# Graph network on one Trainium2 core: the convolution weights' transform with five channels per row block, a separate tile for its difference, and a later fetch of the gates' weights

## The chip, the cores and the metric

The kernel runs on one core of one Trainium2 chip. The metric is the device time of one execution in microseconds (us). TensorE (PE in the profile) multiplies, VectorE (DVE), ScalarE (ACT) and GpSimd (POOL) do the elementwise work, SyncE (SP) issues most loads. Each engine runs its own queue strictly in order; engines meet at semaphores.

## What is computed

The input is 64 graphs of 256 nodes with 256 features each, and a 256x256 adjacency matrix per graph. Layer 0 is a normalised graph convolution with a residual and a layer norm. Layer 1 is, for each graph:

```python
h      = relu(bn1(conv1d(x, conv1_w)))            # one tap
h      = bn2(conv1d(h, conv2_w, pad=8))           # 17 taps, 256 -> 256 channels
x_conv = relu(h + x)
A      = exp(-dist(x @ w_se.T)) * adj
x_nmp  = A @ relu(x @ w_msg.T + b_msg)
x_out  = GRU(input=[x_conv, x_nmp], state=x)      # w_ih, w_hh: the gates
x      = layernorm(x + x_out)
```

Everything is float32. The 17-tap convolution along the nodes is done in frequency space: blocks of 32 nodes, transforms of length 48, one 256x256 matrix of weights per frequency. Only the transform of those weights is touched by the change, apart from the place of one fetch.

## The kernel before, in words

The graphs are taken in four sets of 16 (`Q = 16`, `NQ = 4`). For each set the function `graphs` runs layer 0 and the first part of layer 1 for one graph after another; then `products` multiplies the spectra of all 16 graphs with the weights of each frequency, an inverse transform follows, and `gates` runs the GRU.

The first set has an extra load: while its 16 graphs run, `weights` transforms the 17 taps of `conv2_w` into 24 real frequency rows (`NU = 24`). The taps are put on the partitions: `GC = 4` groups of 64 input channels (`GW = 64`), 17 taps each, so 68 rows (`KT`). A matrix `dft_w` of 68 x 96 columns (24 frequencies x 4 groups), once for the cosine half and once for the sine half, multiplies them. One call of `weights` treats four channels of each group (1024 columns); 16 calls, one per graph, cover all 64. In each call:

- `load_taps` (line 248) fetches the next part into one of two `taps` buffers, with five transfers on SP's queue (lines 257, 258);
- DVE multiplies the taps by the batch-norm scale (line 265);
- PE makes `p_u`, four products of 256 columns for each half (line 272), and ACT copies them into `u_set` (line 275);
- POOL forms the sum of the two halves (line 277) in a third tile, DVE writes the difference over the second tile (line 278), and so has to wait until POOL has read it;
- POOL issues three stores to `ud` in HBM (line 280), 384, 368 and 384 KB.

The generator `weights` yields twice, and `graphs` runs its first half after the transposes of the graph (`p_x1T`, line 387) and its second half after `p_dist` (line 455), by the table `PLACES`. The order of source lines is not the last word: the framework schedules the recorded instructions onto the queues, with priorities and its own idea of when each is ready, and may move an instruction ahead where its inputs permit. Then the order on each engine is fixed.

Other lines that the steps below touch: `layernorm` (lines 290 to 304: DVE statistics, a `pow` on POOL at 293, DVE at 301, ACT at 303), `layer0` (POOL `pow` for the degrees at 329, POOL bias add at 351, DVE at 372), `layer1` (ACT relu of `h` at 400, PE `p_dft` at 431, DVE `dist_r` at 448, PE `p_dist` at 455, DVE `aT` at 457, PE `p_nmp` at 462), `load_u` (line 478, six buffers of 256 KB), `input_sums` (POOL, lines 737 to 740) and `gate_weights` (lines 887, 889, 894). The pools `ustream` and `gate` are opened after the pool `setup` is closed and take over its memory, so their first loads wait for the last users of the setup tiles, among them the `bih` and `bhh` tiles, which reuse the `taps` buffers.

Of the kernel before, what the change touches and what calls it, by code (L numbers as in the profile page):

```python
# [9 lines left out]
F32 = mybir.dt.float32  # L10
AF = mybir.ActivationFunctionType
ALU = mybir.AluOpType
AX = mybir.AxisListType

P = 128
# [11 lines left out]
def kernel(  # L27
# [27 lines left out]
    nc = tc.nc  # L55
    B, N, D = x.shape
    TAPS = conv2T.shape[1]
# [8 lines left out]
    Q = P // GT  # L66
# [3 lines left out]
    const = ctx.enter_context(tc.tile_pool(name="const", bufs=1))  # L70
# [45 lines left out]
    ident = const.tile([P, P], F32)  # L116
# [60 lines left out]
    NF = len(FREQ)  # L177
# [1 line left out]
    RE = (1, 4, 6, 8, 9, 10, 11) + tuple(range(16, 32))  # L179
    IM = (3, 5, 7, 12, 13, 14, 15) + tuple(range(32, 48))  # L180
    NU = NF + 1
    GC = 4
    GW = D // GC
    KT = GC * TAPS
    TR = 16

# [3 lines left out]

    ud = [dram.tile([NU * GC, GW, D], F32, name=f"ud{i}") for i in range(3)]
    fwd = const.tile([P, GT // 2 + 2, FL], F32)
    dft_w = const.tile([KT, 2, NU, GC], F32)

    def tables(pool):
        period = pool.tile([1, 25 * FL], F32, name="period")
        for k in range(FL):
            nc.vector.memset(period[:, k::FL], math.cos(2 * math.pi * k / FL))

        def wave(f, sine, n):  # L200

            first = 0 if not sine else (3 * FL // 4 if f > 0 else FL // 4)
            return period[:, first : first + abs(f) * (n - 1) + 1 : abs(f)]

        fwd_row = pool.tile([1, FL, FL], F32, name="fwd_row")
        w_row = pool.tile([1, TAPS, 2, NU], F32, name="w_row")
        zeros = pool.tile([NT, FL * fm_rows // NT], F32, name="zeros")
        nc.gpsimd.memset(zeros, 0.0)
        nc.gpsimd.dma_start(fm.rearrange("(p r) f -> p (r f)", p=NT), zeros)

        for r in range(2):
            nc.vector.memset(w_row[:, :, r, NF], 0.5)
        nc.vector.memset(w_row[:, 1::2, 1, NF], -0.5)
        for n, f in enumerate(FREQ):
            nc.vector.tensor_copy(w_row[:, :, 0, n], wave(f, False, TAPS))
            nc.vector.tensor_copy(w_row[:, :, 1, n], wave(f, True, TAPS))

        wd = dram.tile([TAPS, 2 * NU], F32, name="wd")
        nc.sync.dma_start(wd.unsqueeze(0), w_row.rearrange("p t h n -> p t (h n)"))
        wt = pool.tile([KT, 2 * NU], F32, name="wt")  # L220
        for c in range(GC):
            nc.sync.dma_start(wt[c * TR : (c + 1) * TR], wd[:TR])
        nc.sync.dma_start(wt[GC * TR :], bcast_rows(wd[TR], 2 * NU, GC))
        mask = pool.tile([KT, GC], F32, name="mask")
        nc.vector.tensor_reduce(
            mask[: GC * TR], ident[: GC * TR, : GC * TR].rearrange("p (c t) -> p c t", c=GC), AX.X, ALU.add
        )
        nc.vector.tensor_copy(mask[GC * TR :], ident[GC * TR : KT, GC * TR : KT])
        nc.vector.tensor_mul(
            dft_w.rearrange("p h n c -> p (h n) c"), wt.unsqueeze(2).to_broadcast([KT, 2 * NU, GC]),  # L230
            mask.unsqueeze(1).to_broadcast([KT, 2 * NU, GC]),
        )

        for r in range(2):
            nc.vector.memset(fwd_row[:, :, 2 * r], 1.0)
        nc.vector.memset(fwd_row[:, 1::2, 2], -1.0)
        for n, f in enumerate(FREQ):
            nc.vector.tensor_copy(fwd_row[:, :, RE[n]], wave(f, False, FL))
            nc.vector.tensor_copy(fwd_row[:, :, IM[n]], wave(-f, True, FL))
        nc.sync.dma_start(fm[fm0 : fm0 + FL].unsqueeze(0), fwd_row)  # L240
        for j in range(GT // 2 + 2):

            first = fm0 + PAD - NT * (j - 1)
            nc.sync.dma_start(fwd[:, j, :], fm[first : first + P])

    TAPS_OF = {}

    def load_taps(pool, n, parts):

        if n == parts:  # L250
            return
        ng = GW // parts
        tp = TAPS_OF[n] = pool.tile([KT, ng, D], F32, name="taps", bufs=2)

        taps = conv2T.rearrange("(c g) t o -> c t g o", c=GC)[:, :, n * ng : (n + 1) * ng]
        for c in range(GC):
            nc.sync.dma_start(tp[c * TR : (c + 1) * TR], taps[c, :TR])
        nc.sync.dma_start(tp[GC * TR :], taps[:, TR])

    def weights(pool, n, parts, scale):  # L260

        ng = GW // parts
        load_taps(pool, n + 1, parts)
        tp = TAPS_OF.pop(n)
        nc.vector.tensor_mul(tp, tp, scale[:KT].unsqueeze(1).to_broadcast([KT, ng, D]))
        m, mf = NU * GC, NF * GC
        us = [pool.tile([m, ng, D], F32, name=f"u_set{i}", bufs=2) for i in range(3)]
        for i in range(2):
            for j in range(0, ng, 2):
                p = accbank("p_u").rearrange("p (g o) -> p g o", g=2)  # L270
                for h in range(2):
                    nc.tensor.matmul(
                        p[:m, h], dft_w[:, i].rearrange("p n c -> p (n c)"), tp[:, j + h], start=True, stop=True
                    )
                nc.scalar.copy(us[i][:, j : j + 2], p[:m])
            if i == 1:
                nc.gpsimd.tensor_tensor(us[2][:mf], us[0][:mf], us[1][:mf], op=ALU.add)
                nc.vector.tensor_sub(us[1][:mf], us[1][:mf], us[0][:mf])
                for d, u, rows in zip(ud, us, (m, m, mf)):
                    nc.gpsimd.dma_start(d[:rows, n * ng : (n + 1) * ng], u[:rows])  # L280
            yield

    def layernorm(y, engine, eps=LN_EPS):
# [192 lines left out]
    def load_u(n, i):  # L476
        u = ustream.tile([P, DCH, D], F32, name="u")
        nc.sync.dma_start(
            u, ud[i][n * GC : (n + 1) * GC].rearrange("c g o -> (c g) o").rearrange("(k p) o -> p k o", p=P)
        )  # L480
        return u

# [385 lines left out]
    with tc.tile_pool(name="setup", bufs=1) as setup:  # L868
        norms = batch_norms(setup)
        next(norms)  # L870
        load_taps(setup, 0, Q)
        nc.sync.dma_start(bmsg_t, bcast_rows(b_msg, D))
        nc.sync.dma_start(bc1[:, D:], bcast_rows(b_se, NSE))
        run(merge(layer0(0), layer0(1)))
        scale2 = next(norms)
        tables(setup)
        load(2)

        def gate_weights():
            for b, half_inputs, cols in ((B11, 0, 0), (T1, 0, 1), (B21, 1, 0), (B22, 1, 1)):  # L880
                at = slice(cols * D, (cols + 1) * D)
                if half_inputs == 0:
                    parts = ((slice(0, DCH), w_hhT), (slice(DCH, HALF), w_ihT[D : D + P]))
# [12 lines left out]

        others = [weights(setup, i, Q, scale2) for i in range(Q)]
        more_weights = gate_weights()
        for i in range(4, 7):
            others[i] = chain(others[i], take(more_weights, 1))  # L900
        run(graphs(0, range(Q), V, others))
        bih_t = setup.tile([P, 3 * D], F32, name="bih", tag="taps", bufs=2)
        nc.sync.dma_start(bih_t, bcast_rows(b_ih, 3 * D))
        bhh_t = setup.tile([P, 3 * D], F32, name="bhh", tag="taps", bufs=2)
        nc.sync.dma_start(bhh_t, bcast_rows(b_hh, 3 * D))
        brz = brz_t.rearrange("p i d -> p (i d)")
        nc.vector.tensor_add(brz, bih_t[:, : 2 * D], bhh_t[:, : 2 * D])
# [127 lines left out]
```

## Time and profile before

| what | value |
|---|---|
| time, median of 3 | 2213.34 us (2213.03 to 2220.08) |
| profiled span | 2214.4 us, granted PE clock 0.986 |
| PE busy | 2077.4 us, 94% of the span |
| DVE / ACT / POOL busy | 71% / 38% / 30% |
| first set of graphs, from first `p_x1T` to `p_x1T` of graph 16 | 36.27 to 345.91 us |
| PE matmul records of `p_u` | 256, of 9853 in all |

Each fp32 matmul of the source stands as two records in the trace, so the 128 products of `p_u` are 256 records. A line of the timeline gives start and duration in us, engine, source line, the operation with its tiles, and in brackets how long the engine sat idle before it and what ended the wait. The sixteen starts of `p_x1T` are used below as the marks that part one graph from the next.

### The profile page before, as it was taken

Reading aid. Unit: us, or ns where it says so; the run is one execution under the profiler, and the core shown is the slowest. Engines: PE = TensorE matmul, PEld = TensorE weight load, DVE = VectorE, ACT = ScalarE, POOL = GpSimd, SP = SyncE. Lnnn points to the kernel's source line nnn. Section 1 sums busy time; section 2 is a strip of 40 time slices with the busy share of each in tenths; the row PEclk is TensorE's granted clock in tenths of the full one; section 3 lists DMA queues with packets and bytes.
Section 4 is the critical chain, followed back from the end, with each engine's and each line's share of the span. In section 5 each row is a group of like instructions: output and inputs, shape, how many; then the busy total and the mean of one; then the engine's idle time right before and its main releaser. Section 6 shows DMA issues by size and latency. Waiting matters only on the chain.

```text
span 2214.4 us, 29080 instructions
## 1 busy us (share of the span) xinstructions
PE 2077.4 (94%) x9853; PEld 1753.5 (79%) x9853; DVE 1564.9 (71%) x3749; ACT 835.9 (38%) x1850; POOL 670.2 (30%) x653
## 2 busy tenths in 40 slices
PE   5999989969999998999999998899999999889998
PEld 4777767848888886788888887688888887678887
DVE  6655448794657899855556989955555879987666
ACT  3555533435441122446543122445554112222222
POOL 2333331113231233322322233321331123344442
PEclk9999999989999999999999999999999999999999
DMA  3655467544337644424334754433323754444342
GB/s 108 193 166 169 150 193 258 170 134 115 118 92 214 200 138 116 132 86 124 105 106 148 214 160 125 143 96 105 119 87 113 216 171 114 115 120 113 102 110 57
DMA packets 251424, 305.20 MB, mean 138 GB/s; under 512 B 18602, under 2 KB 230074, under 8 KB 251275
## 3 DMA queue, kind: packets, MB, share of 16 engines
q1 hardware_dynamic: 183180, 199.85, 29.2%
q10 hardware_dynamic: 45280, 68.04, 8.7%
q0 software_dynamic: 22816, 35.45, 8.1%
q8 instruction: 78, 1.28, 0.2%
q14 instruction: 70, 0.57, 0.1%
HBM read 200.71 MB, written 102.57 MB: 137 GB/s over the span
## 4 chain that ended last, share of the span: by engine, by line
PE 50%; DVE 13%; issue 6%; POOL 5%; ACT 4%; DMA 0%; ACTq 0%; POOLq 0%; SPq 0%; DVEq 0%
PE p_rz L756 18%; PE p_n L793 9%; PE p_k L486 8%; PE p_nmp L462 3%; PE p_out L368 2%; PE p_dft L431 2%; PE p_conv L396 2%; PE p_hT L358 2%; PE p_msg L417 1%; POOL sums L738 1%; POOL ln_rs L293 1%; PE p_dist L455 1%; POOL sums L740 1%; POOL sums L739 1%; DVE gn L798 1%
## 5 line engine op out<-in xcount | busy, mean ns | idle before, releaser
L756 PE MATMUL p_rz<-wrz,sums 128*128 128x256 f32 x1536 | 356.0, 383 | 19.5 <-DVE gn L798 9.8
L793 PE MATMUL p_n<-wn,inputs 128*128 128x256 f32 x1536 | 351.3, 381 | 16.3 <-DVE first L769 15.7
L756 PEld LDWEIGHTS p_rz<-wrz,sums 128*128 128x128 f32 x1536 | 288.6, 191 | 70.9 <-issue 15.8
L793 PEld LDWEIGHTS p_n<-wn,inputs 128*128 128x128 f32 x1536 | 285.7, 190 | 62.2 <-DVE first L769 18.9
L756 PE MATMUL p_rz<-wrz,inputs 128*128 128x256 f32 x1152 | 272.8, 380 | 2.1 <-ACT inputs L728 1.5
L293 POOL TENSOR_TENSOR ln_rs<-ln_rs,neg_half 128x2 f32<-128x2 f32 x129 | 100.4, 778 | 541.3 <-DVE ln_rs L292 455.7
L756 PEld LDWEIGHTS p_rz<-wrz,inputs 128*128 128x128 f32 x1152 | 216.8, 190 | 33.7 <-ACT inputs L728 3.6
L805 ACT ACTIVATE nn<-gn 128x256 f32<-128x256 f32 x128 | 53.2, 416 | 325.6 <-DVE gn L802 324.8
L486 PE MATMUL p_k<-u,VM 128*128 128x256 f32 x736 | 175.1, 380 | 0.8 <-DMA u<-ud 0.8
L329 POOL TENSOR_TENSOR dis<-deg,neg_half 128x2 f32<-128x2 f32 x64 | 49.9, 780 | 403.5 <-DVE deg L327 324.9
L303 ACT ACTIVATE x_g<-x_g,ln_mr,ln_rs 128x256 f32<-128x256 f32 x128 | 70.0, 593 | 256.1 <-DVE ln_mr L301 256.1
L486 PEld LDWEIGHTS p_k<-u,VM 128*128 128x128 f32 x736 | 138.3, 190 | 21.2 <-DMA u<-ud 2.2
L431 PE MATMUL p_dft<-fwd,h 128*128 128x240 f32 x512 | 118.2, 375 | 27.2 <-ACT h L400 27.2
L737 POOL TENSOR_TENSOR sums<-inputs 128x384 f32<-128x384 f32 x64 | 70.0, 1093 | 241.6 <-issue 172.0
L396 PE MATMUL p_conv<-wc,xn 128*128 128x259 f32 x512 | 128.1, 393 | 12.2 <-ACT xn L388 12.2
L358 PE MATMUL p_hT<-adjT,x 128*128 128x256 f32 x512 | 126.8, 392 | 10.0 <-DVE adjT L341 9.3
L431 PEld LDWEIGHTS p_dft<-fwd,h 128*128 128x128 f32 x512 | 95.9, 192 | 44.0 <-ACT h L400 36.4
L462 PE MATMUL p_nmp<-aT,msg 128*128 128x256 f32 x512 | 125.5, 389 | 5.0 <-DVE aT L457 5.0
L368 PE MATMUL p_out<-w,hT 128*128 128x256 f32 x512 | 124.4, 386 | 1.3 <-ACT hT L363 1.1
L396 PEld LDWEIGHTS p_conv<-wc,xn 128*128 128x128 f32 x512 | 98.0, 194 | 31.5 <-ACT xn L388 16.4
L351 POOL TENSOR_TENSOR x_t<-x_t,b_t 128x512 f32<-128x512 f32 x64 | 85.2, 1332 | 121.9 <-ACT x L350 93.2
L417 PE MATMUL p_msg<-wmsg,xn 128*128 128x256 f32 x512 | 122.0, 381 | 0.0
(153 smaller groups left out, 3880.0 us busy)
## 6 DMA issues: line engine op xcount, KB each, us to landing
u<-ud SPq DMA_DIRECT2D x284, 256.0 KB
xn_d<-xn ACTq DMA_DIRECT2D x64, 512.0 KB
inputs<-xn_d SPq DMA_DIRECT2D x64, 512.0 KB
adj_t<-in_adj_dram SPq DMA_DIRECT2D x64, 256.0 KB
x_t<-in_x_dram SPq DMA_DIRECT2D x64, 256.0 KB
x_d<-x ACTq DMA_DIRECT2D x64, 256.0 KB
x_g<-x_d SPq DMA_DIRECT2D x64, 256.0 KB
xc_d<-VM SPq DMA_DIRECT2D x64, 256.0 KB
```

The lines of the kernel that those rows point to most:

```text
L293: nc.gpsimd.tensor_tensor(rs[:, : len(chunks)], rs[:, : len(chunks)], neg_half[:, : len(chunks)], op=ALU.pow)
L303: nc.scalar.activation(y[:, c, :], y[:, c, :], AF.Identity, bias=mr[:, c : c + 1], scale=rs[:, c : c + 1])
L351: nc.gpsimd.tensor_tensor(x_t, x_t, b0_t.unsqueeze(1).to_broadcast([P, NCH, D]), op=ALU.add)
L358: nc.tensor.matmul(p[:, k, :], x1[:, mc, k * P : (k + 1) * P], adjT[:, mc, 1 - mc : 3 - mc, :].rearrange("p n q -> p (n q)"), start=mc == ...
L368: nc.tensor.matmul(p[:, c, :], hT[:, k, c * P : (c + 1) * P], w0[:, k, :], start=k == 0, stop=k == DCH - 1)
L396: nc.tensor.matmul(p, x1T[:, k, c * P : (c + 1) * P], wc1[:, k, :], start=k == 0, stop=k == DCH - 1)
L417: nc.tensor.matmul(p[:, c, :], x1T[:, k, c * P : (c + 1) * P], wmsg[:, k, :], start=k == 0, stop=k == DCH - 1)
L431: nc.tensor.matmul(p[:, t0 * FL : t1 * FL], h[:, c, k * P : (k + 1) * P], fwd[:, first : first + t1 - t0, :].rearrange("p t f -> p (t f)") ...
L462: nc.tensor.matmul(p[:, k, :], msg[:, mc, k * P : (k + 1) * P], aT[:, mc].rearrange("p n q -> p (n q)"), start=mc == 0, stop=mc == NCH - 1,)
L486: nc.tensor.matmul(p[:, j * D : (j + 1) * D], v[:, k, :], u[:, k, :], start=k == 0, stop=k == DCH - 1)
L756: nc.tensor.matmul(p[:, j * D : (j + 1) * D], a[:, k], wrz[:, b, k], start=k == 0, stop=k == HALF - 1)
L793: nc.tensor.matmul(p[:, o * D : (o + 1) * D], lhsT, w, start=j == 0, stop=j == len(part) - 1)
```

## The change

It puts five groups of 52 channels on the rows in place of four groups of 64 (85 rows in place of 68; 120 output rows in place of 96), so that 13 calls of `weights` suffice. The last group has only 48 channels left; its 13th part repeats channels that are not read back. The difference gets a tile of its own (`us[3]`), so DVE need not wait until POOL has read. All 120 rows of sum and difference are stored. To make the plain row (index `NF`) come out right from the difference, its coefficients become 0.5 and 1/0. `dft_w` moves from the constants into the setup pool. `load_taps` now issues seven transfers. The fetch and subtraction of the gates' weights, until now hung onto graphs 4 to 6, take the places 13 to 15, which have no part of `weights` left.

```diff
-    GC = 4
-    GW = D // GC
+    GC = 5
+    GW = 52
+    NPARTS = 13
...
-            nc.vector.memset(w_row[:, :, r, NF], 0.5)
-        nc.vector.memset(w_row[:, 1::2, 1, NF], -0.5)
+            nc.vector.memset(w_row[:, :, r, NF], (0.5, 1.0)[r])
+        nc.vector.memset(w_row[:, 1::2, 1, NF], 0.0)
...
-        ng = GW // parts
+        ng = GW // NPARTS
...
         for c in range(GC):
-            nc.sync.dma_start(tp[c * TR : (c + 1) * TR], taps[c, :TR])
-        nc.sync.dma_start(tp[GC * TR :], taps[:, TR])
+            nc.sync.dma_start(tp[c * TR : (c + 1) * TR], taps(c, 0, TR, 1))
+        nc.sync.dma_start(tp[GC * TR : KT - 1], taps(0, TR, GC - 1, GW * TAPS))
+        nc.sync.dma_start(tp[KT - 1 :], taps(GC - 1, TR, 1, 1))
...
-        us = [pool.tile([m, ng, D], F32, name=f"u_set{i}", bufs=2) for i in range(3)]
+        us = [pool.tile([m, ng, D], F32, name=f"u_set{i}", bufs=2) for i in range(4)]
...
-                nc.gpsimd.tensor_tensor(us[2][:mf], us[0][:mf], us[1][:mf], op=ALU.add)
-                nc.vector.tensor_sub(us[1][:mf], us[1][:mf], us[0][:mf])
-                for d, u, rows in zip(ud, us, (m, m, mf)):
-                    nc.gpsimd.dma_start(d[:rows, n * ng : (n + 1) * ng], u[:rows])
+                nc.vector.tensor_sub(us[3], us[1], us[0])
+                nc.gpsimd.tensor_tensor(us[2], us[0], us[1], op=ALU.add)
+                for d, u in zip(ud, (us[0], us[3], us[2])):
+                    nc.gpsimd.dma_start(d[:, n * ng : (n + 1) * ng], u)
...
-        others = [weights(setup, i, Q, scale2) for i in range(Q)]
         more_weights = gate_weights()
-        for i in range(4, 7):
-            others[i] = chain(others[i], take(more_weights, 1))
+        others = [weights(setup, i, scale2) for i in range(NPARTS)]
+        others += [take(more_weights, 1) for i in range(NPARTS, Q)]
```

More of the change, by code (lines that the diff above doesn't have):

```diff
@@ L192 @@
     fwd = const.tile([P, GT // 2 + 2, FL], F32)
-    dft_w = const.tile([KT, 2, NU, GC], F32)
+    DFT_W = {}
     def tables(pool):
@@ L224, in tables @@
         mask = pool.tile([KT, GC], F32, name="mask")
+        dft_w = DFT_W[0] = pool.tile([KT, 2, NU, GC], F32, name="dft_w")
         nc.vector.tensor_reduce(
-            mask[: GC * TR], ident[: GC * TR, : GC * TR].rearrange("p (c t) -> p c t", c=GC), AX.X, ALU.add
+            mask, ident[:KT, : GC * TR].rearrange("p (c t) -> p c t", c=GC), AX.X, ALU.add
         )
-        nc.vector.tensor_copy(mask[GC * TR :], ident[GC * TR : KT, GC * TR : KT])
+        nc.vector.tensor_add(mask, mask, ident[:KT, GC * TR : KT])
         nc.vector.tensor_mul(
@@ L246, with load_taps, taps, weights @@
     TAPS_OF = {}
-    def load_taps(pool, n, parts):
-        if n == parts:
+    def load_taps(pool, n):
+        if n == NPARTS:
             return
-        ng = GW // parts
+        ng = GW // NPARTS
         tp = TAPS_OF[n] = pool.tile([KT, ng, D], F32, name="taps", bufs=2)
-        taps = conv2T.rearrange("(c g) t o -> c t g o", c=GC)[:, :, n * ng : (n + 1) * ng]
-        for c in range(GC):
-            nc.sync.dma_start(tp[c * TR : (c + 1) * TR], taps[c, :TR])
-        nc.sync.dma_start(tp[GC * TR :], taps[:, TR])
-    def weights(pool, n, parts, scale):
-        ng = GW // parts
-        load_taps(pool, n + 1, parts)
+        def taps(c, t, count, step):
+            channel = min(c * GW + n * ng, D - ng)
+            return bass.AP(
+                tensor=conv2T.tensor, offset=conv2T.offset + (channel * TAPS + t) * D,
+                ap=[[step * D, count], [TAPS * D, ng], [1, D]],
+            )
+        for c in range(GC):
+            nc.sync.dma_start(tp[c * TR : (c + 1) * TR], taps(c, 0, TR, 1))
+        nc.sync.dma_start(tp[GC * TR : KT - 1], taps(0, TR, GC - 1, GW * TAPS))
+        nc.sync.dma_start(tp[KT - 1 :], taps(GC - 1, TR, 1, 1))
+    def weights(pool, n, scale):
+        ng = GW // NPARTS
+        load_taps(pool, n + 1)
         tp = TAPS_OF.pop(n)
         nc.vector.tensor_mul(tp, tp, scale[:KT].unsqueeze(1).to_broadcast([KT, ng, D]))
-        m, mf = NU * GC, NF * GC
-        us = [pool.tile([m, ng, D], F32, name=f"u_set{i}", bufs=2) for i in range(3)]
+        m = NU * GC
+        us = [pool.tile([m, ng, D], F32, name=f"u_set{i}", bufs=2) for i in range(4)]
         for i in range(2):
@@ L272, in weights @@
                     nc.tensor.matmul(
-                        p[:m, h], dft_w[:, i].rearrange("p n c -> p (n c)"), tp[:, j + h], start=True, stop=True
+                        p[:m, h], DFT_W[0][:, i].rearrange("p n c -> p (n c)"), tp[:, j + h], start=True, stop=True
                     )
@@ L478, in load_u @@
         nc.sync.dma_start(
-            u, ud[i][n * GC : (n + 1) * GC].rearrange("c g o -> (c g) o").rearrange("(k p) o -> p k o", p=P)
+            u, ud[i][n * GC : (n + 1) * GC].rearrange("c g o -> (c g) o")[:D].rearrange("(k p) o -> p k o", p=P)
         )
@@ L870 @@
         next(norms)
-        load_taps(setup, 0, Q)
+        load_taps(setup, 0)
         nc.sync.dma_start(bmsg_t, bcast_rows(b_msg, D))
```

## The prediction, made before the changed kernel ran

> **What bounds the kernel now.** I read the page first: PE is busy 94% of the span, so time falls where PE gets less work or waits less. The change touches the first set of graphs alone. The built order of the changed program agrees: after the first set's products, PE's queue is the same instruction for instruction. So I cut the first 346 us at the starts of `p_x1T` of graphs 3, 13, 14, 15 and 16 and asked for the sums by window.
>
> ```profile
> core 0: us, PE busy (x) PEld busy (x) DVE busy (x) ACT busy (x) POOL busy (x), PEclk, DMA share, GB/s
> 90.20:262.30 172.10, 159.78 (x782) 128.34 (x780) 86.97 (x230) 98.77 (x230) 66.73 (x71) 1.00 0.52 161
> 262.30:279.47 17.17, 15.97 (x79) 12.84 (x78) 8.80 (x23) 9.88 (x23) 6.67 (x8) 1.00 0.52 161
> 279.47:297.20 17.73, 15.38 (x65) 11.50 (x64) 10.04 (x22) 9.54 (x22) 8.46 (x10) 0.88 0.61 192
> 297.20:345.91 48.71, 42.60 (x186) 34.36 (x184) 25.44 (x58) 13.09 (x29) 7.67 (x8) 0.94 0.72 234
> ```
>
> Ten steady graphs take 17.2 us each with PE 93% busy; graph 14 no less, though it has no layer 0 beside it; the last window loses clock too. What `p_u` costs PE stands in the groups of the first 480 us:
>
> ```profile
> L272 PE MATMUL p_u<-taps,dft_w 68*96 68x256 f32 x256 | 62.9, 387 | 0.0
> ```
>
> Then the timeline of one steady graph, cut to the loop that carries it:
>
> ```profile
> 243.43 2.35 POOL L277 TENSOR_TENSOR u_set<-u_set,u_set 92x1024 f32<-92x1024 f32 x1
> ...
> 245.82 1.22 DVE L278 TENSOR_TENSOR u_set<-u_set,u_set 92x1024 f32<-92x1024 f32 x1 [1.67 <-POOL u_set L277]
> ...
> 246.96 0.47 DVE L372 SCALAR_TENSOR_TENSOR x<-p_out,dis,x_t 128x256 f32<-128x256 f32 x1
> ...
> 248.60 0.71 POOL L293 TENSOR_TENSOR ln_rs<-ln_rs,neg_half 128x2 f32<-128x2 f32 x1 [0.74 <-DVE ln_rs L292]
> ...
> 249.54 1.09 ACT L303 ACTIVATE x<-x,ln_mr,ln_rs 128x256 f32<-128x256 f32 x2 [3.15 <-DVE ln_mr L301]
> ...
> 251.55 0.63 ACT L400 ACTIVATE h<-h 128x512 f32<-128x512 f32 x1
> ...
> 252.23 1.89 PE L431 MATMUL p_dft<-fwd,h 128*128 128x240 f32 x8 [0.86 <-ACT h L400]
> ...
> 254.51 1.38 DVE L265 TENSOR_TENSOR taps<-taps,scale 68x1024 f32<-68x1024 f32 x1 [1.21 <-DMA taps<-in_conv2T_dram]
> ...
> 256.41 0.70 PE L455 MATMUL p_dist<-dist_r,dist_l 32*128 32x256 f32 x4 [0.34 <-DVE dist_r L448]
> ```
>
> Two waits stop PE in a graph. `p_dft` waits 0.86 us: POOL's sum, DVE's difference, the layer norm queued behind both, ACT's normalisation, and only then ACT's relu. `p_dist` waits 0.34 us (0.28 to 0.53) because the taps' multiply stands in DVE's queue ahead of `dist_r` and waits for its transfer. Last, the end of the set:
>
> ```profile
> 307.29 2.34 POOL L277 TENSOR_TENSOR u_set<-u_set,u_set 92x1024 f32<-92x1024 f32 x1 [5.39 <-ACT u_set L275]
> ...
> 308.17 2.00 DVE L457 TENSOR_TENSOR aT<-aT,adjT 128x512 f32<-128x512 f32 x1 [1.06 <-ACT aT L456]
> ...
> 310.23 3.60 PE L462 MATMUL p_nmp<-aT,msg 128*128 128x256 f32 x8 [2.96 <-DVE aT L457]
> ...
> 311.60 0.63 POOL L280 DMA_DIRECT2D ud<-u_set  x1 [1.15 <-DVE u_set L278]
> ...
> 315.65 15.03 SPq L478 DMA_DIRECT2D u<-ud  x16
> ...
> 321.35 1.97 PE L486 MATMUL p_real<-u,VM 128*128 128x256 f32 x8 [1.17 <-DMA u<-ud]
> ```
>
> The weights are stored only after 311.6, so their first load is issued at 315.65 and the products start at 321.35, with little for PE to do before. One row of the waits matters as well:
>
> ```profile
> POOL sums L737 <- DMA x_g<-x_d: 22.6, 1, 22.6
> ```
>
> The first sum of the gates is queued on POOL long before its inputs are loaded, and holds up all behind it.
>
> **What the Trainium skill says.** "SBUF — State Buffer", section "SBUF: two separate sides": DVE and GpSimd share one port pair, a lock held for the whole instruction, when the DVE instruction has two SBUF inputs; whoever starts first keeps it. The trace agrees: `aT`, 0.69 us at 258.01, takes 2.00 at 308.17 and ends 0.54 us after POOL's sum. "TensorE: Matmul & The Clock Gate", section "Part 1": PE's clock halves after idling. The trace agrees: eight records of `p_nmp` take 1.89 us in the steady graphs and 3.60 after a wait of 2.96.
>
> **The change part by part.**
>
> *Fewer products.* A product's time is set by its 256 columns: eight records take 1.89 us with 68x96 as with 128x128. 128 products become 104, so 24 x 62.9/128 = 11.8 us of PE busy time go (start to start 0.43, so 10.3 when PE is dense). They leave graphs 13 to 15, where they partly filled waits.
>
> *Steady graphs.* The built order puts the taps' multiply behind `dist_r`: the 0.34 goes, and `dist_r` to `aT` has room for its 1.22 us (`aT` waits for ACT anyway; `p_nmp` has 1.7 us of slack behind `p_u` and `p_out`). The seven transfers add some 0.8 us of issue, hidden, as `x_t` before them is freed 1.7 us earlier. The difference no longer waits by semaphore, but still by the lock. It becomes ready at 243.0, while POOL's `pow` (line 329) runs to 243.45; POOL's sum is next. If DVE goes first (as at 430 us in the trace, where a DVE instruction in the same position won), the difference ends at 244.75 and the sum at about 247.0. Then two stores at 0.29 + 0.58 and 0.1 + 0.52, and `pow` starts at 248.6: as now, since today's second store waits for the difference and `pow` for the statistics. So the path from `p_dist` to the next `p_dft` stays at 13.0 us (239.23 to 252.23), and that from `p_dft` to `p_dist` falls from 4.2 to 3.67. Period 16.7 instead of 17.2: -0.5, for nine graphs -4.5 us. Should DVE lose, the layer norm, now behind the difference, starts 0.8 us later: period 17.45, +0.27 per graph.
>
> *Gates' weights.* Despite their new place in the source, the built order still has their loads during graphs 2 to 4, and the four subtractions (0.96 us each) around graph 3, two of them just ahead of the difference; before, they cost graph 2 some 0.9 us. I take +1.5 net (0 to 3).
>
> *Graph 13* has no `p_u`, but waits for the copy to `xn` (about 1.0): `p_dft` 6.2 us after `p_x1T`, then 8.0: 14.2 instead of 17.17, -3.0.
>
> *Graph 14.* By its chain alone: `p_x1T` to `p_conv` 1.5, to `p_dft` 5.0, wait for `dist_r` 1.3, for `aT` 1.75: 12.4 us. But in the built order the gates' first sum (line 737) now stands on POOL ahead of the layer norm's `pow` of graph 15, whose ACT step stands ahead of this graph's relu. Its inputs are loaded behind six loads of `u`, which wait for the last store of the weights, 8 us after `p_x1T` of graph 13. From there some 2.4 MB at the 276 GB/s that 310 to 340 us shows: 8.6 us, and 2 for latency: 19 us. Sum 1.0, `pow` 0.7, DVE 0.2, ACT 1.1 and 0.63: `p_dft` at 23.5, which is 9.3 into graph 14 instead of 5.0. With 4.3 us more and one or two half-clock stretches (1.8 each): 18.5 to 20, against 17.73: +1.5.
>
> *Graph 15 and the start of the products.* PE's work from here to `p_x1T` of graph 16: 75 products of 0.43, and 5.6 us of smaller work: 37.9 us, measured 48.7. After: five products fewer, 35.7, and the first `p_real` and `p_k` fill the waits of graph 15, because the weights are long stored. I leave 4 us for waits: 39.7, -9.0.
>
> Stores grow from 1136 to 1440 KB a part, for 13 instead of 16: the same bytes in total, at a DMA share of 0.52, hidden. The conversions of `w_row` and the mask cost nothing: PE waits for layer 0 then.
>
> Sum: -4.5 + 1.5 - 3.0 + 1.5 - 9.0 = -13.5 us: 2199.8.
>
> **The rivals.** *A, this sum*, 50%. *B, everything frees PE*: the lock is held only briefly by `pow`, the sum ends earlier, the steady period falls to 16.2 (-9 us), and the inputs land before graph 14 needs them (-4 instead of +1.5): 2213.3 - 9 + 1.5 - 3 - 4 - 9 = 2190. For it: `pow` has only two elements a row. Against: POOL's queue is full end to end in that stretch. 20%. *C, DVE loses the lock*: +2.4 instead of -4.5: 2206.7. For it: at 45.3 us a DVE instruction lost to this very sum. Against: that one came 0.05 us ahead of the handover, this one 0.4. 20%. *D, slower*: C, and POOL's sum blocks some 8 us longer, graph 14 at +8 and graph 15 at half clock for most of its length, -3: +2.4 + 1.5 - 3 + 8 - 3 = +6, 2219. For it: before, the same sum blocked POOL for 22.6 us. Against: this time only six loads stand ahead. 10%.
>
> **How the numbers follow.** The likeliest is A, 2200. The range reaches from B, a little below, to above C: 2187 to 2211. Faster than 2206.7: A nearly whole, B, half of C: 0.80. Within 0.3%: the other half of C and some of A: 0.13. Slower: most of D, 0.07.
>
> **What would show it.** Steady marks of `p_x1T` 16.7 apart, the wait of `p_dist` gone, that of `p_dft` about 1.0; POOL's sum starting after DVE's difference; a wait of `p_dft` of some 4 us in graph 14, ended by ACT behind POOL's line of gates' sums; `p_real` inside graph 15. Wrong it would be with a steady period of 17.4, with `p_real` still after the set, or with a different time after graph 16, where I expect the same length to the end.

## The result, and the profile after

The changed kernel takes 2197.26 us (median of four, 2192.67 to 2198.09) against 2213.26 us for the kernel before on the same chip. The ratio is 0.9916, with an interval of 0.9893 to 0.9939: 16 us less. The forecast was 2200, its working 2199.8. The total is near; several of its terms are not, and two of them are wrong by more than the whole of that difference.

First the sums by window of the changed kernel, cut at the same marks as before (starts of `p_x1T` of graphs 3, 13, 14, 15 and 16):

```profile
core 0: us, PE busy (x) PEld busy (x) DVE busy (x) ACT busy (x) POOL busy (x), PEclk, DMA share, GB/s
91.85:255.48 163.63, 159.53 (x782) 131.30 (x781) 92.27 (x235) 98.65 (x230) 74.04 (x71) 1.00 0.64 201
255.48:268.93 13.45, 12.68 (x64) 10.23 (x62) 7.70 (x25) 7.85 (x19) 4.45 (x5) 1.00 0.80 243
268.93:290.70 21.77, 13.14 (x43) 9.55 (x42) 4.07 (x18) 7.12 (x17) 4.30 (x5) 0.69 0.42 149
290.70:328.56 37.86, 37.01 (x175) 31.27 (x174) 22.61 (x56) 12.79 (x28) 3.36 (x4) 1.00 0.63 189
```

In the ten steady graphs PE does the same work (159.5 us) in 163.6 us instead of 172.1, with the DMA share up from 0.52 to 0.64. Graph 14 is longer than before, with PE at 0.69 of its clock. The last window is 11 us shorter. The fewer products stand in the groups of the first 480 us, 52.3 us instead of 62.9, at nearly the same time for each (396 and 387 ns):

```profile
L283 PE MATMUL p_u<-taps,dft_w 85*120 85x256 f32 x208 | 52.3, 396 | 1.7 <-DVE dft_w L231 1.7
```

Then the timeline of one steady graph, the loop that was shown of before (lines are about eleven higher: POOL's sum is L289, the difference L288, `pow` of the degrees L340, `pow` of the layer norm L304):

```profile
220.97 0.71 POOL L340 TENSOR_TENSOR dis<-deg,neg_half 128x2 f32<-128x2 f32 x1 [4.70 <-DVE deg L338]
221.20 1.23 DVE L288 TENSOR_TENSOR u_set<-u_set,u_set 120x1024 f32<-120x1024 f32 x1
...
221.67 2.97 POOL L289 TENSOR_TENSOR u_set<-u_set,u_set 120x1024 f32<-120x1024 f32 x1
222.46 0.88 DVE L383 SCALAR_TENSOR_TENSOR x<-p_out,dis,x_t 128x256 f32<-128x256 f32 x2
...
226.07 0.73 POOL L304 TENSOR_TENSOR ln_rs<-ln_rs,neg_half 128x2 f32<-128x2 f32 x1
...
227.03 1.10 ACT L314 ACTIVATE x<-x,ln_mr,ln_rs 128x256 f32<-128x256 f32 x2 [2.39 <-DVE ln_mr L312]
...
229.77 1.89 PE L442 MATMUL p_dft<-fwd,h 128*128 128x240 f32 x8 [0.15 <-ACT h L411]
...
233.54 0.70 PE L466 MATMUL p_dist<-dist_r,dist_l 32*128 32x256 f32 x4
```

DVE's difference no longer waits. It starts while `pow` runs and takes its usual 1.23 us. POOL's sum starts 0.47 us later and is the one that is held up: 2.97 us instead of 2.35, ending 2.2 us after the difference. `p_dft` waits 0.15 us instead of 0.86, and the wait of `p_dist` is gone.

The end of the set, in the timeline of graphs 13 to 15:

```profile
264.41 2.93 SPq L489 DMA_DIRECT2D u<-ud  x6
...
274.57 0.99 POOL L748 TENSOR_TENSOR sums<-inputs 128x384 f32<-128x384 f32 x1 [11.11 <-DMA x_g<-x_d]
...
276.19 0.71 POOL L304 TENSOR_TENSOR ln_rs<-ln_rs,neg_half 128x2 f32<-128x2 f32 x1
...
277.13 0.60 ACT L314 ACTIVATE x<-x,ln_mr,ln_rs 128x256 f32<-128x256 f32 x1 [6.93 <-DVE ln_mr L312]
...
278.67 0.63 ACT L411 ACTIVATE h<-h 128x512 f32<-128x512 f32 x1 [0.44 <-DVE scols L420]
279.35 3.56 PE L442 MATMUL p_dft<-fwd,h 128*128 128x240 f32 x8 [5.34 <-ACT h L411]
...
287.13 3.78 PE L473 MATMUL p_nmp<-aT,msg 128*128 128x256 f32 x8 [1.65 <-DVE aT L468]
...
297.74 1.53 PE L497 MATMUL p_real<-u,VM 128*128 128x256 f32 x6
```

The weights are loaded from 264.41 on instead of 315.65, and `p_real` runs inside graph 15. The price stands in between: the first of the gates' sums, moved ahead on POOL, waits 11.11 us for its inputs; the layer norm's `pow` is queued behind it, ACT's normalisation waits for that, the relu is queued behind the normalisation, and PE stands still for 5.34 us and then runs `p_dft` and `p_nmp` at half clock (3.56 and 3.78 us where the steady graphs have 1.89).

By stage, in us, all from the marks of the profiled executions (the third row is an experiment below):

| kernel | start to graph 1 | graphs 1, 2 | 3 to 12 | 13 | 14 | 15 and products | graph 16 to end | span |
|---|---|---|---|---|---|---|---|---|
| before | 55.46 | 34.74 | 172.10 | 17.17 | 17.73 | 48.71 | 1868.5 | 2214.4 |
| after | 59.20 | 32.65 | 163.63 | 13.45 | 21.77 | 37.86 | 1866.8 | 2195.4 |
| `e7_both_late` | 55.90 | 32.66 | 160.26 | 13.57 | 13.39 | 38.16 | 1867.3 | 2181.2 |

### The profile page after: what moved, and what is told of

Read it like the earlier page. It is cut to its first block, busy times and chain, and to the rows that moved or that the text cites. A ratio compares the mean times of both kernels' runs of the same rounds, so it can differ in the third digit from the quotient of the medians.

```text
span 2195.4 us, 28939 instructions
## 1 busy us (share of the span) xinstructions
PE 2070.3 (94%) x9805; PEld 1754.5 (80%) x9805; DVE 1554.1 (71%) x3743; ACT 828.8 (38%) x1838; POOL 664.1 (30%) x641
## 4 chain that ended last, share of the span: by engine, by line
PE 50%; DVE 14%; issue 6%; POOL 6%; ACT 4%; DMA 0%; ACTq 0%; POOLq 0%; SPq 0%; DVEq 0%
PE p_rz L767 18%; PE p_n L804 9%; PE p_k L497 8%; PE p_nmp L473 2%; PE p_out L379 2%; PE p_dft L442 2%; PE p_conv L407 2%; PE p_hT L369 2%; POOL sums L749 1%; POOL ln_rs L304 1%; PE p_msg L428 1%; PE p_dist L466 1%; POOL sums L751 1%; POOL sums L750 1%; DVE gn L809 1%
## 5 line engine op out<-in xcount | busy, mean ns | idle before, releaser
L804 PEld LDWEIGHTS p_n<-wn,inputs 128*128 128x128 f32 x1536 | 285.8, 190 | 61.8 <-DVE first L780 18.5
L304 POOL TENSOR_TENSOR ln_rs<-ln_rs,neg_half 128x2 f32<-128x2 f32 x129 | 100.3, 777 | 538.9 <-DVE ln_rs L303 453.1
L340 POOL TENSOR_TENSOR dis<-deg,neg_half 128x2 f32<-128x2 f32 x64 | 48.5, 758 | 428.8 <-DVE deg L338 322.7
```

The source lines that it names most:

```text
L304: nc.gpsimd.tensor_tensor(rs[:, : len(chunks)], rs[:, : len(chunks)], neg_half[:, : len(chunks)], op=ALU.pow)
L804: nc.tensor.matmul(p[:, o * D : (o + 1) * D], lhsT, w, start=j == 0, stop=j == len(part) - 1)
```

## The experiments

**Theory and rivals.** Theory: the steady gain comes from the own tile alone, because DVE's difference, and the layer norm behind it, no longer wait for POOL's sum; the 24 products that are gone pay only at the end of the set; two pieces of gates' work that stand too early in the queues (the four subtractions in graph 4, the first sum in graph 14) give some 11 us back. Rivals: the products make the whole gain; the port that DVE and POOL share holds the difference back as long as the semaphore did; the loads set the end of the set anyway.

The place of the fetch of the gates' weights can be left out of this: with `more_weights` chained to graphs 4 to 6 again, the built order of the changed program is the same, instruction for instruction, on all five engines. That edit does nothing.

**1. The own tile alone.**

```diff
 # the kernel before (4 channels, 16 parts)
-    nc.vector.memset(w_row[:, :, r, NF], 0.5)
+    nc.vector.memset(w_row[:, :, r, NF], (0.5, 1.0)[r])
-nc.vector.memset(w_row[:, 1::2, 1, NF], -0.5)
+nc.vector.memset(w_row[:, 1::2, 1, NF], 0.0)
...
-    nc.gpsimd.tensor_tensor(us[2][:mf], us[0][:mf], us[1][:mf], op=ALU.add)
-    nc.vector.tensor_sub(us[1][:mf], us[1][:mf], us[0][:mf])
+    nc.vector.tensor_sub(us[3], us[1], us[0])
+    nc.gpsimd.tensor_tensor(us[2], us[0], us[1], op=ALU.add)
```

> The kernel before with one thing of the change: the difference gets a tile of its own and is recorded ahead of POOL's sum (with it go the plain row's coefficients 0.5, 1 and 0, and all 96 rows in sums and stores). Four channels on the rows, 16 parts and 128 products stay. Theory, own tile: most of the steady gain is the wait of p_dft, 0.86 us in a graph before and 0.10 after the whole change. It goes here too, while the wait of p_dist (0.34 us) stays, since the taps' multiply still stands ahead of dist_r: steady marks 16.4 us apart instead of 17.2, graphs 14 and 15 nearly as before, 0.8 x 12 = 10 us, about 2203. Rival, fewer products: the gain comes from the 24 products that are gone and from the early end of the weights; then this kernel takes 2213 (2211 to 2215), steady marks 17.2. Second rival, the lock: DVE has to wait for POOL's sum now through the shared port instead of a semaphore, steady marks 17.2 to 17.5, 2213 to 2217.

Measured: 2203.45 us (2202.39 to 2207.58), ratio to before 0.9951 (0.9939 to 0.9963). The sums by window of its graphs 3 to 12, and its timeline at the same place:

```profile
94.11:254.03 159.92, 159.06 (x781) 128.35 (x780) 87.89 (x231) 98.83 (x230) 81.41 (x71) 1.00 0.54 174
```

```profile
228.39 1.89 PE L431 MATMUL p_dft<-fwd,h 128*128 128x240 f32 x8
...
229.46 1.22 DVE L265 TENSOR_TENSOR taps<-taps,scale 68x1024 f32<-68x1024 f32 x1
...
235.66 0.71 POOL L329 TENSOR_TENSOR dis<-deg,neg_half 128x2 f32<-128x2 f32 x1 [3.85 <-DVE deg L327]
235.89 1.22 DVE L277 TENSOR_TENSOR u_set<-u_set,u_set 96x1024 f32<-96x1024 f32 x1
...
236.36 2.98 POOL L278 TENSOR_TENSOR u_set<-u_set,u_set 96x1024 f32<-96x1024 f32 x1
```

Ten graphs in 159.92 us with PE busy 159.06: the list of PE's waits has no row for that stretch. The period is 16.0, even below the 16.4 expected, because the wait of `p_dist` went too, though the taps' multiply still stands ahead of `dist_r`: it no longer waits for its transfer. SP issues that transfer behind the one into `x_t`, and `x_t` is freed by the instruction queued behind the difference (L372), which now runs earlier: in the kernel before it ends at 247.43 and the transfer into `x_t` is issued at 247.50, 4.7 us ahead of `p_dft`; here they stand at 238.02 and 238.08, 6.3 us ahead of it. So both waits go with the own tile. The rival of fewer products is out for the steady graphs, since here there are 128 of them. The end of the set is hardly shortened: graph 14 takes 14.1 us instead of 17.7, but graph 15 with the products 51.1 instead of 48.7.

**2. The parts alone.**

```diff
 # the changed kernel
-us = [pool.tile([m, ng, D], F32, name=f"u_set{i}", bufs=2) for i in range(4)]
+us = [pool.tile([m, ng, D], F32, name=f"u_set{i}", bufs=2) for i in range(3)]
...
-    nc.vector.tensor_sub(us[3], us[1], us[0])
     nc.gpsimd.tensor_tensor(us[2], us[0], us[1], op=ALU.add)
+    nc.vector.tensor_sub(us[1], us[1], us[0])
```

> The changed kernel with the difference written over the second half's tile again, behind POOL's sum; five channels on the rows, 13 parts, 104 products stay. Theory, own tile: the wait of p_dft comes back, 0.7 to 0.9 us in each of the twelve graphs that carry a part; the wait of p_dist stays gone: steady marks 16.8 apart, 2197 + 0.8 x 12 = 2206 to 2207. Rival, fewer products: the own tile is worth nothing, 2197 (2195 to 2199), steady marks 16.0 to 16.1.

Measured: 2211.52 us (2208.14 to 2218.28), ratio 0.9987 (0.9980 to 0.9993): 3 us less than before, 5 more than the theory had. The waits of its PE queue from 94 to 270 us, each row with the sum in us, how often and the longest:

```profile
PE p_dft L442 <- ACT h L411: 12.7, 10, 2.2
```

The wait of `p_dft` is back. Graphs 5 to 12 take 17.1 us each on average, just as before the change, so 13 parts on 85 rows are worth next to nothing there. The list has no row for `p_dist`: with `dist_r` ahead of the taps' multiply its wait is gone here too, but `p_dft` waits longer. Graphs 3 and 4 take 18.5 and 20.7, where the gates' subtractions stand (109.1 to 117.8 us; the first takes 2.97 us beside POOL's sum); this is what I hadn't counted. What the parts alone give is graph 15 and the products, 38.2 us instead of 48.7, most of it lost again in graphs 3, 4 and 14 (1.3, 3.5 and 3.3 us more than before). The two halves of the change are worth 11 and 3 us alone and 16 to 17 together.

**3. The first of the gates' sums held back.**

```diff
 # the changed kernel, input_sums
-    nc.gpsimd.tensor_tensor(S[:, 2], A11, A21, op=ALU.subtract)
     nc.gpsimd.tensor_tensor(S[:, 0], A21, A22, op=ALU.add)
+    if g == 0:
+        nc.gpsimd.tensor_copy(S[0:1, 2, 0, 0:1], S[0:1, 0, 0, 0:1])
+    nc.gpsimd.tensor_tensor(S[:, 2], A11, A21, op=ALU.subtract)
```

> The changed kernel, in which the first of the gates' sums (A11 - A21 of graph 0) can't be moved ahead on POOL: it is recorded behind the second sum, and one element is copied from the second sum's result into its tile first, so it waits for that. Theory, the blocked queue: in graph 14 POOL waits 11.1 us for this sum's inputs, the layer norm and ACT's relu stand behind it, p_dft waits 5.3 us and p_nmp then runs at half clock. Without it graph 14 takes 13 to 14 us instead of 21.8, and half of that may come back as a wait for loads at the products: 2189 to 2193. Rival, the loads set the end anyway: the products are limited by the loads of u, graph 14 is shorter but p_real and p_k wait for it: 2196 to 2198. Second rival, the sums late: the four gates' sums, now all late, hold up the gates of the first graphs of the second set, 2199 or more.

Measured: 2194.08 us (2186.14 to 2194.89), ratio 0.9894 (0.9879 to 0.9908). The windows of its graph 14 and of graph 15 with the products:

```profile
271.52:285.37 13.85, 10.40 (x44) 8.17 (x43) 4.38 (x18) 6.97 (x17) 3.36 (x4) 0.88 0.66 228
285.37:323.13 37.76, 36.86 (x176) 31.11 (x175) 22.62 (x56) 12.79 (x28) 3.38 (x4) 1.00 0.61 189
```

Graph 14 takes 13.85 us instead of 21.77, and the products after it are no longer: the blocked queue was the whole of that loss, and the rival that the loads set the end is out. The time is just above the 2189 to 2193 of the theory, and its five values fall into two groups (2186.1 and 2188.8; 2194.1 to 2194.9). In the profile 2.8 us are lost again after graph 16. Of these, 1.2 stand in graphs 19 to 24 (graph 22 takes 36.3 us against 35.1 in the profile of the result). The second rival, that the late sums hold up the gates, could be behind that, but isn't shown: the four sums come together only in graph 23, at 490 to 495 us. The other 1.6 us stand in graph 32, which takes 33.6 us or 35.2 to 35.3 in the profiles here whatever the edit.

**4. The gates' subtractions held back.**

```diff
 # the changed kernel, gate_weights
+    nc.vector.tensor_copy(wrz[0:1, T3, 0, 0:1], V[0:1, 0, 0, 12 * GT : 12 * GT + 1])
     for to, a, b in ((T3, B22, T1), (T1, T1, B11), (T2, B22, T1), (T4, B21, T2)):
```

> The changed kernel, in which the four subtractions of the gates' weights wait for data of graph 12: one element of its spectrum is copied into the first result's tile ahead of them, so they can't be moved ahead to graph 3; the loads stay early. Theory: the graph of 19.1 us (16.0 in its neighbours) has its 3.1 us from these subtractions, the first of which took 3.04 us beside POOL's sum, and in graphs 13 to 15 nothing waits for them: 2197 - 3 = 2194. Rival: the 3.1 us are the seven loads of the gates' weights (1.8 MB) that take bandwidth from taps and x: 2197, still one graph of 19.

Measured: 2190.40 us (2189.71 to 2192.22), ratio 0.9890 (0.9876 to 0.9904). Graph 4 takes 15.66 us instead of 19.14, with the loads of the weights where they were, so the loads are not the cause. The time lies 4 us below the theory; its profile has the first graph at full clock (19.5 us instead of 24.2), which experiment 5 takes up. What happened in the changed kernel, from its timeline:

```profile
105.36 2.35 POOL L289 TENSOR_TENSOR u_set<-u_set,u_set 120x1024 f32<-120x1024 f32 x1 [4.57 <-ACT u_set L286]
105.48 4.04 DVE L905 TENSOR_TENSOR wrz<-wrz 128x768 f32<-128x768 f32 x2 [1.21 <-DMA wrz<-in_w_ihT_dram]
...
109.43 1.22 DVE L288 TENSOR_TENSOR u_set<-u_set,u_set 120x1024 f32<-120x1024 f32 x1
...
117.35 1.89 PE L442 MATMUL p_dft<-fwd,h 128*128 128x240 f32 x8 [2.42 <-ACT h L411]
```

Two subtractions stand ahead of the difference; the first starts 0.12 us behind POOL's sum and is held until that ends (4.04 us for two, where two others took 0.93 and 0.95). The difference and the layer norm come 4 us late, and `p_dft` waits 2.42 us.

**5. The changed kernel again, as a neighbour for the next ones.**

> The changed kernel unaltered, as the neighbour of the next kernels on the same chip. The graphs' first 24.2 us in its profile (19.2 before) hold a stretch of some 10 us at half clock; e5_gate_subs_late, with the same waits of PE there, ran it at full clock and took 19.5. Theory: the stretch comes and goes from run to run whatever the kernel, so the times here fall into two groups some 5 us apart, about 2192 with a clock of 0.986 and 2197 with 0.982, and the change's own cost at the start is at most 0.5 us. Rival: the change's wait for dft_w (1.71 us) brings it on each time, all times near 2197, clock 0.981 or 0.982.

Measured: 2197.74 us (2193.48 to 2200.66), ratio 0.9918 (0.9903 to 0.9932). Two of the five times are 2193.5 and 2193.8 with a clock of 0.985, three are 2197.7 to 2200.7 with 0.981 or 0.982: two groups, as the theory had it. That they differ in the start alone is not shown; in the two profiles of this kernel the start to graph 1 differs by 2.5 us and graph 14 by 1.4 (21.77 and 20.37), and graph 22 takes 35.1 us in one and 32.7 in the other, behind the same waits of PE (9.56 and 5.25 us), as half clock lasts longer in the first. Some 4 us of a difference between medians here can come from this. How PE's first graph differs, from the changed kernel and from `e5_gate_subs_late`, which has the same work and the same waits there:

```profile
37.20 3.82 PE L407 MATMUL p_conv<-wc,xn 128*128 128x259 f32 x8 [0.67 <-ACT xn L399]
42.73 3.77 PE L283 MATMUL p_u<-taps,dft_w 85*120 85x256 f32 x8 [1.71 <-DVE dft_w L231]
```

```profile
38.56 2.02 PE L407 MATMUL p_conv<-wc,xn 128*128 128x259 f32 x8 [0.68 <-ACT xn L399]
42.29 1.99 PE L283 MATMUL p_u<-taps,dft_w 85*120 85x256 f32 x8 [1.71 <-DVE dft_w L231]
```

The same instructions behind the same waits run at half clock in one and at full clock in the other.

**6. Both pieces held back.**

```diff
 # the changed kernel, with the line of experiment 4 and
+    tie = const.tile([1, 1], F32)
...
     run(graphs(0, range(Q), V, others))
+    nc.gpsimd.tensor_copy(tie, V[0:1, FL - 1, 0, (Q - 1) * GT : (Q - 1) * GT + 1])
...
+    if g == 0:
+        nc.gpsimd.tensor_copy(S[0:1, 2, 0, 0:1], tie)
     nc.gpsimd.tensor_tensor(S[:, 2], A11, A21, op=ALU.subtract)
```

> The changed kernel with both hoisted pieces made to wait: the gates' four subtractions for data of graph 12 as in e5_gate_subs_late, the first of the gates' sums for one element of graph 15's spectrum (instead of for the second sum, as in e4_first_sum_late, which gave 7.9 us back in graph 14 but ended only some 3 us earlier). Theory: both gains add up: graph 4 at 15.7 us, graph 14 at 13.8, and with the first sum ahead of the second again nothing is lost later: 11 us less than the changed kernel, 2182 to 2186. Rival: the loss after the first set in e4_first_sum_late (about 2.8 us by its profile) lies in the shifted stages and not in the order of the sums; then 2186 to 2189.

Measured: 2183.33 us (2180.64 to 2184.10), ratio 0.9853 (0.9840 to 0.9865): 14 us below its neighbour of experiment 5, with no overlap of times; no version here is faster. Its windows:

```profile
88.56:248.82 160.26, 159.03 (x782) 131.36 (x780) 91.23 (x236) 98.76 (x230) 73.93 (x71) 1.00 0.65 205
248.82:262.39 13.57, 12.80 (x63) 10.22 (x62) 7.67 (x26) 7.86 (x19) 4.57 (x5) 1.00 0.80 250
262.39:275.78 13.39, 9.95 (x44) 7.77 (x43) 4.38 (x18) 6.98 (x17) 3.37 (x4) 0.91 0.67 234
275.78:313.94 38.16, 37.31 (x175) 31.41 (x174) 22.61 (x56) 12.83 (x28) 5.63 (x7) 0.99 0.60 187
```

Graph 4 and graph 14 both give back what they had cost: 3.5 and 8.4 us against the profile of the result, 3.5 and 7.0 against that of experiment 5, so 10.5 to 11.9 us of the 14. Graphs 19 to 21 and 24 take what they take in the changed kernel, so that part of the loss in experiment 3 is gone with the first sum recorded ahead of the second again. Graph 22 doesn't tell: it takes 32.7 us here and 35.1 in experiment 7, with the sums in the same order.

**7. `dft_w` built on POOL as well.**

```diff
 # e7_both_late
-        nc.vector.tensor_mul(
+        nc.gpsimd.tensor_tensor(
             dft_w.rearrange("p h n c -> p (h n) c"), wt.unsqueeze(2).to_broadcast([KT, 2 * NU, GC]),
-            mask.unsqueeze(1).to_broadcast([KT, 2 * NU, GC]),
+            mask.unsqueeze(1).to_broadcast([KT, 2 * NU, GC]), op=ALU.mult,
         )
```

> e7_both_late with the multiplication that builds dft_w on POOL, which is idle there, instead of on DVE behind h. PE's 1.71 us wait for dft_w goes. Theory: 0.3 to 1.7 us less than e7_both_late, since PE waits for DVE's adjT later in that graph anyway; and if the wait is what halves the clock, all runs at 0.985 or more. Rival: POOL's product is slow and takes DVE's port from the sums of h: the same as e7_both_late or 1 us more.

Measured: 2183.79 us (2180.16 to 2185.31), ratio 0.9853 (0.9840 to 0.9866): the same as `e7_both_late`, so the theory's gain of 0.3 to 1.7 us is not there. The wait of `p_u` for `dft_w` is gone, and graph 0 takes 19.67 us although `p_conv` ran at half clock there, but graphs 3 and 4 take 2.0 us more: the taps' multiply waits 2.78 us for a transfer at 100.4 us, where SP took 3.87 us to issue three transfers of taps instead of 1.40 in `e7_both_late`. Why it took longer is open. All clocks are 0.985 or more, but so are those of `e7_both_late`, which has the wait; this doesn't tell whether the wait halves the clock.

**8. The difference made to wait for `pow`.**

```diff
 # the changed kernel
     nc.gpsimd.tensor_tensor(dis, deg, neg_half[:, :NCH], op=ALU.pow)
+    DIS[0] = dis
...
+    nc.vector.tensor_copy(us[3][0:1, 0, 0:1], DIS[0][0:1, 0:1])
     nc.vector.tensor_sub(us[3], us[1], us[0])
```

> The changed kernel in which DVE first copies one element of the result of POOL's pow for the degrees (line 340), and only then forms the difference. In the changed kernel the difference ran at its full speed through that pow (221.20 to 222.43 beside 220.97 to 221.68) and POOL's sum, started at 221.67, took 2.97 us instead of 2.35. The prediction had the pow holding the difference back until its end. Theory: after the pow POOL's sum starts first, DVE loses and forms the difference only at its end, 2.4 us later than now; with it go the layer norm and the relu ahead of p_dft, so steady marks 17.2 to 17.5 us apart and 12 x 1.3 = 16 us more, 2210 to 2213. Rival, the prediction's own step: DVE waits for the pow and then still goes first; steady marks 16.0 to 16.7, 2197 to 2204.

Measured: 2213.78 us (2211.94 to 2218.91), ratio 0.9994 (0.9985 to 1.0003). The marks alternate between 17.1 and 18.4 us, 17.7 on average, above the 17.2 to 17.5 expected. Its timeline:

```profile
234.63 0.71 POOL L341 TENSOR_TENSOR dis<-deg,neg_half 128x2 f32<-128x2 f32 x1 [4.70 <-DVE deg L339]
...
235.33 2.35 POOL L290 TENSOR_TENSOR u_set<-u_set,u_set 120x1024 f32<-120x1024 f32 x1
235.38 0.14 DVE L288 COPY u_set<-dis 1x1 f32<-1x1 f32 x1 [0.53 <-POOL dis L341]
235.45 3.31 DVE L289 TENSOR_TENSOR u_set<-u_set,u_set 120x1024 f32<-120x1024 f32 x1
```

Started 0.12 us behind the sum, the difference is held until the sum ends (237.68) and finishes at 238.76. The whole gain of the change is gone. It hangs on the difference coming ahead of the sum, by 0.47 us in the changed kernel.

**9. A longer `pow`.**

```diff
 # the changed kernel
-        dis = small.tile([P, NCH], F32, name="dis")
-        nc.gpsimd.tensor_tensor(dis, deg, neg_half[:, :NCH], op=ALU.pow)
+        dis_w = small.tile([P, NCH, 24], F32, name="dis")
+        nc.gpsimd.tensor_tensor(
+            dis_w, deg.unsqueeze(2).to_broadcast([P, NCH, 24]),
+            neg_half[:, :NCH].unsqueeze(2).to_broadcast([P, NCH, 24]), op=ALU.pow,
+        )
+        dis = dis_w[:, :, 0]
```

> The changed kernel in which POOL's pow for the degrees (line 340) writes 24 copies of each result, 48 elements a row instead of 2; all else and the order on every engine in the steady graphs is the same. The difference on DVE becomes ready about 0.2 us after this pow has started. Question: does pow never hold DVE's difference back, or was it only too small. Theory, too small: with 48 elements the pow lasts 0.9 to 3 us, DVE's difference takes longer than 1.23 us when it starts within it, and where the pow ends last, POOL's sum may go first as in e9_wait_for_pow: marks 16.5 to 17.7 us apart, 2203 to 2214. Rival, pow doesn't contend with DVE: the difference takes 1.23 us inside the pow, and POOL's sum starts later by what the pow is longer; with the 0.1 to 0.5 us of room in the path that follows, marks 16.0 to 16.6 apart, 2197 to 2205.

Measured: 2508.93 us, ratio 1.1327 (1.1308 to 1.1346); graphs 24 to 26 us apart, far outside both expectations of time, as `pow` lasts 8.03 us and not 0.9 to 3. The question itself is settled by its timeline:

```profile
261.15 8.03 POOL L340 TENSOR_TENSOR dis<-deg,neg_half 128x48 f32<-128x48 f32 x1 [6.80 <-DVE deg L338]
261.54 1.23 DVE L288 TENSOR_TENSOR u_set<-u_set,u_set 120x1024 f32<-120x1024 f32 x1
...
269.16 2.33 POOL L289 TENSOR_TENSOR u_set<-u_set,u_set 120x1024 f32<-120x1024 f32 x1
```

The difference lies wholly inside an 8 us `pow` and takes 1.23 us. A `pow` that has started doesn't hold DVE back, however long; POOL's sum does. The other way round `pow` is held too, in graph 4 of the changed kernel:

```profile
112.35 0.93 DVE L905 TENSOR_TENSOR wrz<-wrz 128x768 f32<-128x768 f32 x1
112.42 1.43 POOL L340 TENSOR_TENSOR dis<-deg,neg_half 128x2 f32<-128x2 f32 x1 [0.94 <-DVE deg L338]
```

Here DVE's subtraction of two tiles came first, and `pow` takes 1.43 us instead of 0.71, ending 0.57 us after the subtraction.

## Why the prediction was right or wrong

The sum, term by term, from the stage table (graph 4 apart, 17.17 before and 19.14 after):

| term | predicted | profile |
|---|---|---|
| nine steady graphs | -4.5 | -10.4 |
| gates' subtractions (graphs 1, 2 and 4) | +1.5 | -0.1 |
| graph 13 | -3.0 | -3.7 |
| graph 14 | +1.5 | +4.0 |
| graph 15 and products | -9.0 | -10.9 |
| start to graph 1 | 0 | +3.7 |
| after graph 16 | 0 | -1.7 |
| sum | -13.5 | -19.0 |

- **Steady graphs: the step that failed is "The difference no longer waits by semaphore, but still by the lock", where it has `pow` hold the lock until 243.45.** I let that `pow` hold the difference back, and so kept the wait of `p_dft` at about 1.0 us; it is 0.15. `pow` doesn't hold it (experiment 9); the difference starts at once, the sum with its stores ends earlier, and `pow` of the layer norm starts in time. From `p_dist` to the next `p_dft` it is 12.3 us and not 13.0. The order I took (difference first) was right, the period of 16.7 was not: 16.03. The rival that frees PE had this part right. The trace of before shows it at the place that the prediction cites:

```profile
428.77 1.68 POOL L329 TENSOR_TENSOR dis<-deg,neg_half 128x2 f32<-128x2 f32 x1 [18.79 <-DVE deg L327]
...
430.01 1.21 DVE L536 SCALAR_TENSOR_TENSOR VM<-VM 128x1024 f32<-128x1024 f32 x1
```

  DVE's instruction starts 0.44 us before the `pow` ends and takes 1.21 us, about what the difference of as many columns takes undisturbed (1.22): it had not waited for the `pow` (which took 1.68 us, as another instruction of DVE, 428.70 to 429.89, had come first). The Trainium skill, "SBUF — State Buffer", section "SBUF: two separate sides", gives the lock to whichever starts first, against a GpSimd operation that reads SBUF. The sums and subtractions of this case agree (3.31 us in experiment 8; only at 45.31 us before the change does a DVE instruction lose that started 0.03 us ahead of the sum), and so does a `pow` that comes second (1.43 us instead of 0.71); a `pow` that comes first, and reads SBUF too, does not (1.23 us inside 8.03), so the measurement decides.
- **The other rival's cost, DVE losing**, was sized at 17.45 us a graph; made to lose, it is 17.7. That mechanism was right, and the changed kernel escapes it.
- **The wait of `p_dist`** went, as predicted. The new order of the taps' multiply is reason enough, as experiment 2 shows; what the prediction didn't see is that the own tile is too, by the earlier transfer (experiment 1).
- **Gates' subtractions.** They cost 3.1 us in graph 4 (19.14 beside 16.03 in its neighbours; 3.5 against experiment 4), and free the 0.9 us of graph 2: +2.2, within the 0 to 3 given. That the row reads -0.1 is the steady gain in graphs 2 and 4, about 1.15 us each, which "for nine graphs" left out.
- **Graph 14: mechanism right, size somewhat too small.** The inputs arrive at 274.57, 19.1 us after `p_x1T` of graph 13 (predicted 19), and `p_dft` starts 10.4 us into the graph (predicted 9.3). The prediction has `p_dft` at 23.5 us, but what it lists adds up to 22.6; measured are 23.9, since `pow` of the degrees (0.71) stands in that chain too and the relu waits 0.44 us for `scols` on DVE. The other term that was mis-sized is what follows: 11.3 us from there to `p_x1T` of graph 15, with PE at 0.69 of its clock, where 18.5 to 20 for the whole graph left 9 to 11. Without the block the graph takes 13.4 (experiment 6), with `p_dft` 4.9 into it, as the prediction's chain had it (5.0). So the block costs 8.4 us, and I had 6 to 7.6. In the profile of experiment 5 the same graph takes 20.37 us and the block costs 7.0, so part of the miss is the clock.
- **Graph 15 and the products** came within 2 us: the waits were less than the 4 us left for them, PE being busy 37.01 of 37.86 us.
- **The start** was set at nothing, and the profile shows +3.7. The wait for `dft_w`, now behind `h` in DVE's queue, was overlooked, but it costs at most some 0.5 us: `e7_both_late` has it and reaches graph 1 only 0.44 us later than before. The rest is the half clock of the first graph, which comes and goes with the same waits. The Trainium skill, "TensorE: Matmul & The Clock Gate", section "Part 1", says that the window over which activity is judged runs free of the kernel, so that the same work starts cold for a different length each time. The trace agrees: 3.82 us for `p_conv` in seven of the eleven profiles here, 2.02 in four. Whether the 1.71 us wait makes the half clock last longer isn't settled; it lasted through the first eight records of `p_u` in two of the eight profiles with it (3.77 us), and in none of the three without.
- **After graph 16** the products continue with loads that began earlier: 28.7 us to graph 17 instead of 30.2, a gain I had put at nothing. A different time there was one of the prediction's own signs of being wrong.

That the total came out so near is luck, since the errors have both signs: of the gain, 5.9 us were missed in the steady graphs, 1.6 in the row of the subtractions, 0.7 in graph 13, 1.9 in graph 15 and 1.7 later; of the loss, 2.5 in graph 14 and 3.7 at the start. (The two profiled executions differ by 19.0 us, the medians by 16.0.)

## What to carry to other kernels

When two engines read the same tile and one of them overwrites it, give the result a tile of its own and let the short operation go first: here that alone was worth 11 us without removing any work, while removing 24 products from PE alone gave 3, as most of what that saves was lost again to pieces that stood too early. Look at every instruction that the built order has moved ahead of its neighbours in a queue, and ask when its data arrive: two such pieces cost 10.5 to 11.9 us together, and one element copied from the data of a later graph was enough to put them in their place. An order that is won by half a microsecond should be written down and measured from both sides, since losing it took the whole gain.

## What was unexpected in the hardware

- POOL's `pow` takes 0.71 us for 128x2 and 8.03 us for 128x48, so by these two sizes 0.16 us for each further element of a row, while POOL's add of 120x1024 takes 2.33 to 2.35 us in all.
- This `pow` leaves DVE's two-input difference alone (1.23 us inside it), while the add holds the same difference until its own end (3.31 us when started 0.12 us behind it), and is itself held by the difference when that is first (2.97 us instead of 2.35). A `pow` that starts behind a DVE instruction with two SBUF inputs is held as well (1.43 us instead of 0.71). So `pow` yields to DVE and never holds it in these traces; why is not shown.
